# Two-layer cross attention: four context transfers under way instead of eight, one context block in another buffer, a small matrix product placed later

## The chip, the cores and the metric

The kernel runs on one core of one Trainium2 chip, in 32-bit floats. The metric is device time in microseconds (us) of one execution; the median of three executions before the change is 591.29 us (590.97 to 593.39). Engine names are those of the profile: PE multiplies matrices, PEld loads its weights, DVE, ACT and POOL work on vectors, SP issues most of the DMA transfers.

## The reference, cut to what matters

Eight batches (B) of 100 queries (T) with 1024 features (E) attend to a context of 1444 rows (S) with 512 features (L), in two layers one after the other. Layer 0 has an output projection and a softmax over the context; layer 1 has a softmax over the queries, no output projection, and a layer norm.

```python
def _L0_xattn_ref(query, key, Wq, bq, Wk, bk, Wv, bv, Wo, bo):
    Q = jnp.einsum('bqd,dh->bqh', query, Wq) + bq
    K = jnp.einsum('bkd,dh->bkh', key, Wk) + bk
    V = jnp.einsum('bkd,dh->bkh', key, Wv) + bv
    scores = jnp.einsum('bqh,bkh->bqk', Q, K) * scale
    weights = jax.nn.softmax(scores, axis=-1)
    attended = jnp.einsum('bqk,bkh->bqh', weights, V)
    return query + jnp.einsum('bqh,hd->bqd', attended, Wo) + bo

def _L1_xattn_ref(emb, latent, Wq, bq, Wk, bk, Wv, bv, gamma, beta):
    ...
    w = jax.nn.softmax(w, axis=1)
    pred = jnp.einsum('btm,bme->bte', w, v)
    x = pred + emb
    ...
    return (x - mu) * jax.lax.rsqrt(var + EPS) * gamma + beta
```

## The kernel before

**The algebra.** The kernel never forms keys or values. It multiplies Wq by Wk once (qk0 for layer 0, qk1 for layer 1) and Wv by Wo (vo0), with seven half-size products where eight would be plain (`weight_products`, L350). From qk0 and the queries it makes g0T (`queries`, L657), so that the scores of a batch are g0T times the context itself. The weighted context rows A are then projected: `project0` (L1041) after layer 0, `project1` (L1194) and `project_last` in layer 1.

**The context comes twice per batch and layer.** `load_features` (L862) brings it transposed, as four feature blocks cT_b_0 to cT_b_3 of 128 features by 1444 rows, each in two transfers (704 and 740 columns; the page lists them as 352 and 370 KB). `load_rows` (L871) brings it as it lies, as four pieces c_b_0 to c_b_3 of three blocks of 128 rows each: eleven transfers of 256 KB, and for the last 36 rows one of 72 KB and one of 64 KB. So a batch needs 21 transfers. All go through `loaded_in_order` (L859), which issues them on SP's queue in the order of the program. Completion is told by eight semaphores in turn, so each transfer is issued only after the eighth before it has landed: up to eight are under way.

**Buffers.** The pool `stream` (L60) holds ten units; a unit takes one piece c_b_q, or one of the blocks cT_b_0 and cT_b_1. Blocks cT_b_2 and cT_b_3 go to three buffers with the tag prob (`feature_block`, L86). A transfer into a buffer also waits until PE is through with what was in it. Before the context, the units hold the weights for qk1.

**The order on PE** is written out by hand. `scores_by_keys` (L941, matmuls at L957) goes through the four feature blocks of a batch, and in each through the twelve row blocks in the order KEYS (8, 11, 9, 10, 0 to 7), so the second half of a block is wanted first. `weighted_rows` (L902, matmuls at L910) makes A of a batch from the pieces c in order. `alternated` (L1318) runs A of batch b and the scores of batch b+2 step by step in turn; the scores of batches 0 and 1 run ahead of it. The sequence of layer 0 stands at L1330 to L1368: loads for batches 0, 1 and partly 2, the scores of batch 0, further loads, the scores of batch 1, then eight rounds of `alternated`; the first two parts of `project0` run after the seventh round, the rest after the eighth. Layer 1 begins with `queries(1, ...)`, the scores of its batches 0 and 1 (L1394 to L1399), and runs `alternated` in three sets (batches 0 to 3, 4 to 6, and 7) with a projection after each.

**DVE, ACT and POOL** are scheduled by the framework, except where `vector.in_order` or `keep_in_program_order` holds them to the program's order. `softmax0` (L981) and `softmax1` (L1125) work on the scores of one batch while PE is at the next ones.

**The small product.** Layer 1's bias vectors are sums over weights (`block_sums`, L590). `totals("k1", ...)` (L601, matmul at L604) multiplies those partial sums by a matrix of zeros and ones, `same`, to add them over the partitions; DVE then masks and adds (L607, L609). Its results u1 and wqbk1 are used by `queries(1, ...)` (L1355) and `key_bias_sums` (L1373). It stands at L1364, at the end of round b = 1, just ahead of `value_sums` (L1367), which prepares sums of wvo for `project0` on DVE.

Of the kernel before, what the change touches and what calls it, by code (L numbers as in the profile page):

```python
# [34 lines left out]
S, L = 1444, 512  # L35
EC, LC = E // P, L // P
# [13 lines left out]
PAD = S - LAST + QD  # L50
SCALE = 1.0 / math.sqrt(E)
EPS = 1e-6


@with_exitstack
def two_layer_cross_attention(ctx: ExitStack, tc: tile.TileContext, a: dict, out: bass.AP):
    nc = tc.nc
# [10 lines left out]
    def bank(name):  # L68
        return psum.tile([P, 512], F32, tag="ps", name=name)
# [4 lines left out]
    def unit(name):  # L74
        return stream.tile([P, E + L], F32, tag="unit", name=name)

    def wide(name):
        return work.tile([P, LC, GT], F32, tag="AT", name=name, bufs=2)
# [7 lines left out]
    def feature_block(name):  # L86
        return work.tile([P, S], F32, tag="prob", name=name, bufs=3)
# [55 lines left out]
    def run(*parts):  # L143

        parts = list(parts)
        while parts:
            parts = [g for g in parts if next(g, parts) is not parts]
# [442 lines left out]
    def block_sums(name, t, sums, late=False):  # L590

        ins = nc.vector.transpose(t, t)
        if late:
            tc.keep_in_program_order(ins)
        nc.vector.tensor_reduce(sums, t.rearrange("p (c q i) -> p c q i", q=P // QD, i=QD), AX.X, ALU.add)

    def totals(name, sums, n):  # L601

        ps = bank(name)[:, : n * P // QD]
        nc.tensor.matmul(ps, same, sums.rearrange("p c q -> p (c q)"), start=True, stop=True)  # L604
        own = small.tile([P, 2 * EC, P // QD], F32, tag="own", name=f"{name}_own", bufs=1)[:, :n, :]
        mask = quarter.unsqueeze(1).to_broadcast([P, n, P // QD])
        nc.vector.tensor_tensor(own, ps.rearrange("p (c q) -> p c q", q=P // QD), mask, ALU.mult)  # L607
        got = const.tile([P, n], F32, tag=name, name=name)
        nc.vector.tensor_reduce(got, own, AX.X, ALU.add)  # L609
        return got  # L610

    def quarter_sums(name):
        return small.tile([P, 2 * EC, P // QD], F32, tag="sums", name=f"{name}_sums")
# [14 lines left out]
    def key_bias_sums(name, wqbk, tiles=()):  # L628

        acc = to = work.tile([P, B * T], F32, tag="kb", name=name, bufs=1)

        def steps():
            if tiles:
                scaled_sum(tiles, [(xT[:, k, :], wqbk[:, k : k + 1]) for k in range(EC)])
            for k in range(len(tiles), EC):
                if k == len(tiles):
                    vector.tensor_scalar(to, xT[:, k, :], wqbk[:, k : k + 1], None, ALU.mult)  # L640
                else:
                    vector.scalar_tensor_tensor(to, xT[:, k, :], wqbk[:, k : k + 1], to, ALU.mult, ALU.add)
                yield
            if tiles:
                transfer_added(to, tiles[0])

        return acc, steps()
# [178 lines left out]
    for g in range(B // G):  # L826
# [3 lines left out]
                out=xT[:, :, g * GT : (g + 1) * GT],  # L830
                in_=a["xT"].rearrange("(c p) t -> p c t", p=P)[:, :, g * GT : (g + 1) * GT],
# [16 lines left out]
    kb0, more = key_bias_sums("kb0", wqbk0[:, :EC], [t[:, : B * T] for t in prob])  # L848
# [3 lines left out]
    sums = quarter_sums("k1")  # L852
# [3 lines left out]
        tc.keep_in_program_order(nc.scalar.activation(xT[:, e, :], xT[:, e, :], AF.Identity, bias=bias))  # L856


    def loaded_in_order(to, src):  # L859
        tc.keep_in_program_order(nc.sync.dma_start(out=to, in_=src))  # L860

    def load_features(b):  # L862

        for k in range(LC):
            name = f"cT_{b}_{k}"
            t = feature_block(name) if k >= LC // 2 else unit(name)[:, :S]
            for part in (slice(0, LAST // 2), slice(LAST // 2, S)):
                loaded_in_order(t[:, part], a["ctxT"][b][k * P : (k + 1) * P, part])
            yield t

    def load_rows(b):  # L871

        src = a["ctx_512"][b]
        for q in range(NQ):
            t = unit(f"c_{b}_{q}").rearrange("p (c l) -> p c l", c=CQ)
            n = CQ - (q == NQ - 1)
            r0 = q * CQ * P
            for i in range(n):
                loaded_in_order(t[:, i, :], src[r0 + i * P : r0 + (i + 1) * P, :])
            if n < CQ:  # L880
                more = PAD - (S - LAST)
                loaded_in_order(t[: S - LAST, n, :], src[LAST:S, :])
                loaded_in_order(t[S - LAST : PAD, n, :], src[:more, :])
            yield t
# [56 lines left out]
    def scores_by_keys(s, layer, cT, softmax):  # L941

        b = s["b"]
        q = gT[layer][b // G]
        t0 = b % G * T
        banks = [bank(f"s{layer}_{b}_{n}") for n in range(MC // GM)]
        rest = []
        for k in range(LC):
            for m in KEYS:
                whole = keys(m) == P  # L950
                n = HP if whole else keys(m)
                for h in both_sides() if whole else one_side():
                    o = m * P + h * HP if whole else m * P
                    to = banks[m // GM][h * HP : h * HP + n, m % GM * T : (m % GM + 1) * T]
                    if k >= LC - 2 and not whole:
                        rest.append(to)
                    nc.tensor.matmul(  # L957
                        to,
                        cT[k][:, o : o + n],
                        q[:, k, t0 : t0 + T],  # L960
                        start=(k == 0 and m % GM == 0),
                        stop=(k == LC - 1 or (k == LC - 2 and not whole)),
                        skip_group_check=True,
                    )
                if (k, m) != (LC - 1, KEYS[-1]):
                    yield
        w = weight_rows(f"w{layer}_{b}")
        s["w"] = w[:, : MC * T].rearrange("p (c t) -> p c t", t=T)
        nc.gpsimd.memset(s["w"][:PAD, MC - 1, :], 0.0)  # L969
        s["softmax"] = softmax(s, [blocks_of(banks, ms) for ms in ROWS], rest)  # L970
        for _ in islice(s["softmax"], LATER.get((layer, b))):
            pass
        yield
# [257 lines left out]
    def normalise(s):  # L1231
# [6 lines left out]
        rstd = small.tile([T, 1], F32, tag="rstd", name=f"rstd_{b}")  # L1238
        nc.vector.tensor_scalar(rstd, mv[:, 1:2], EPS, None, ALU.add)
        nc.gpsimd.tensor_tensor(rstd, rstd, mhalf[:T], ALU.pow)  # L1240
# [19 lines left out]
    def project_last(s, A, first):  # L1260
# [31 lines left out]
        vector.tensor_tensor(v, sq[:, 0:1], sq[:, 1:2], ALU.add)  # L1292
        vector.tensor_scalar(v, v, 1.0 / E, EPS, ALU.mult, ALU.add)
        for part in parts[1:]:
# [23 lines left out]
    def alternated(b, layer, softmax, dst, first=0, got=None):  # L1318
# [6 lines left out]
        for _ in range(MC * LC):  # L1325
            next(A)
            next(ahead, None)
            yield

    loads = [load_features(b) for b in range(3)]  # L1330
    cT = [list(islice(load, n)) for load, n in zip(loads, (LC, LC - 1, 0))]
    c0 = list(load_rows(0))
    cT[2] += islice(loads[2], LC // 2)
    run(scores_by_keys(batches[0], 0, cT[0], softmax0))
    cT[1] += loads[1]
    cT[2] += islice(loads[2], 1)
    block_sums("u1", acc_u, sums[:, :LC, :], late=True)
    block_sums("wqbk1", acc_c, sums[:, LC : LC + EC, :], late=True)
    run(scores_by_keys(batches[1], 0, cT[1], softmax0))
    cT[2] += loads[2]  # L1340
    for b in range(B):
        dst = A0[b // G][:, :, b % G * T : (b % G + 1) * T]
        steps = alternated(b, 0, softmax0, dst, *((0,) if b else (MC, (c0, cT[2]))))
        if b == B - 2:
            o0 = project0(AS, A0)
            parts = [next(o0), next(o0)]
        if b < B - 1:
            run(steps)
        if b == B - 2:
            vector.in_order = True  # L1350
            for part in parts:
                run(part)
            vector.in_order = False
        if b == B - 1:
            gT[1], queries1 = queries(1, wqk1, u1)  # L1355
            for n, _ in enumerate(steps):
                if n in (7, 11, 15):
                    vector.in_order = True
                    next(queries1)
                    vector.in_order = False  # L1360
        for e in range(2 * b, 2 * b + 2) if 2 * b < EC else ():
            add_out_bias(e)
        if b == 1:
            got = totals("k1", sums[:, : LC + EC, :], LC + EC)  # L1364
            u1, wqbk1 = got[:, :LC], got[:, LC:]
            vector.in_order = True
            AS = value_sums(wvo)  # L1367
            vector.in_order = False  # L1368
# [4 lines left out]
    kb1, more = key_bias_sums("kb1", wqbk1)  # L1373
# [29 lines left out]
    for bs in SETS:  # L1403
        t = wide(f"A1T_{bs[0]}").rearrange("p c t -> p (c t)")[:, : LC * len(bs) * T]
        t = t.rearrange("p (c t) -> p c t", c=LC)
# [42 lines left out]
```

## Time and profile before

| what | value |
|---|---|
| median of three executions | 591.29 us (590.97 to 593.39) |
| profiled execution, its own time | 592.69 us |
| span of its trace, first to last instruction | 590.9 us |
| mean granted TensorE clock | 0.996 |
| PE busy | 575.6 us (97%) |
| DMA, mean over the span | 242 GB/s, 142.95 MB |
| context transfers (c and cT) | 336 of the issues, all on SP's queue |

The profile is of one execution. Busy time is the union of an engine's instructions; matmuls are pipelined, so that their recorded durations overlap. "Idle before" names what ended an engine's idle time: an instruction of another engine, a DMA, or "issue", where the profile shows nothing that it waited for. Queue q1 carries the transfers that SP issues, q0 those of POOL, and q8 and q14 bring instructions to the engines.

### The profile page before, as it was taken

Reading aid. Unit: us, or ns where it says so; the run is one execution under the profiler, and the core shown is the slowest. Engines: PE = TensorE matmul, PEld = TensorE weight load, DVE = VectorE, ACT = ScalarE, POOL = GpSimd, SP = SyncE. Lnnn points to the kernel's source line nnn. Section 1 sums busy time; section 2 is a strip of 40 time slices with the busy share of each in tenths; the row PEclk is TensorE's granted clock in tenths of the full one; section 3 lists DMA queues with packets and bytes.
Section 4 is the critical chain, followed back from the end, with each engine's and each line's share of the span. In section 5 each row is a group of like instructions: output and inputs, shape, how many; then the busy total and the mean of one; then the engine's idle time right before and its main releaser. Section 6 shows DMA issues by size and latency. Waiting matters only on the chain.

```text
span 590.9 us, 17499 instructions
## 1 busy us (share of the span) xinstructions
PE 575.6 (97%) x7470; PEld 497.1 (84%) x7470; DVE 398.9 (68%) x936; ACT 133.1 (23%) x349; POOL 132.2 (22%) x206
## 2 busy tenths in 40 slices
PE   9999999999999899999999999999989999999994
PEld 8887457678899899999997666787989999999992
DVE  1997589879675963966559597867434447654695
ACT  1331421423420112121111000203333302154313
POOL 3110110221211222141223002205722112341052
PEclk9999999999999999999999999999999999999998
DMA  8959989943699999999972607609999992599124
GB/s 271 311 120 328 300 211 295 259 84 84 118 262 355 343 369 359 369 341 378 352 226 58 245 0 269 225 22 381 345 336 347 355 342 72 157 320 308 48 29 84
DMA packets 65097, 142.95 MB, mean 242 GB/s; under 512 B 7549, under 2 KB 12925, under 8 KB 65021
## 3 DMA queue, kind: packets, MB, share of 16 engines
q1 hardware_dynamic: 56574, 117.80, 56.9%
q0 software_dynamic: 8048, 23.57, 19.1%
q8 instruction: 59, 0.97, 0.7%
q10 hardware_dynamic: 398, 0.47, 0.2%
q14 instruction: 18, 0.14, 0.1%
HBM read 121.53 MB, written 6.14 MB: 216 GB/s over the span
## 4 chain that ended last, share of the span: by engine, by line
PE 89%; DMA 6%; issue 2%; POOL 2%; ACT 1%; DVE 0%; POOLq 0%; DVEq 0%
PE A L910 21%; PE s L957 20%; PE qk_x L166 6%; PE g_x L166 5%; PE o_x L166 5%; PE vo_x L166 4%; DMA cT<-in_ctxT 3%; PE o_y L166 3%; DMA c<-in_ctx 3%; PE g_y L166 3%; PE qk_y L166 2%; PE qk_z L166 2%; PE o_w L166 1%; PE o_z L166 1%; PE qk_w L166 1%
## 5 line engine op out<-in xcount | busy, mean ns | idle before, releaser
L910 PE MATMUL A<-w,c 128*64 128x100 f32 (+1 forms) x3072 | 228.4, 249 | 0.9 <-issue 0.9
L910 PEld LDWEIGHTS A<-w,c 128*64 128x64 f32 (+1 forms) x3072 | 198.9, 137 | 4.4 <-issue 4.1
L957 PE MATMUL s<-g1T,cT 128*64 128x100 f32 (+1 forms) x1472 | 114.5, 249 | 2.3 <-issue 2.2
L957 PE MATMUL s<-g0T,cT 128*64 128x100 f32 (+1 forms) x1472 | 112.8, 249 | 3.6 <-DMA cT<-in_ctxT 1.9
L957 PEld LDWEIGHTS s<-g1T,cT 128*64 128x64 f32 (+1 forms) x1472 | 98.5, 136 | 4.7 <-issue 4.0
L957 PEld LDWEIGHTS s<-g0T,cT 128*64 128x64 f32 (+1 forms) x1472 | 96.5, 136 | 4.3 <-DMA cT<-in_ctxT 2.1
L1169 POOL TENSOR_TENSOR part<-w 128x500 f32<-128x500 f32 x16 | 23.8, 1486 | 124.9 <-ACT w L1017 61.9
L1149 ACT ACTIVATE w<-w,negmax 128x100 f32<-128x100 f32 x96 | 35.0, 366 | 71.1 <-DVE negmax L99 71.1
L99 DVE SCALAR_TENSOR_TENSOR w<-s,kb 128x400 f32<-128x400 f32 (+2 forms) x32 | 13.9, 463 | 40.3 <-PE s L957 40.1
L1017 ACT ACTIVATE w<-w 128x400 f32<-128x400 f32 (+2 forms) x32 | 12.0, 442 | 123.0 <-DVE w L99 123.0
L99 DVE TENSOR_REDUCE most<-s 128x100 f32<-128x400 f32 (+1 forms) x24 | 12.5, 522 | 39.7 <-PE s L957 39.6
L166 PE MATMUL qk_x<-qk 128*128 128x256 f32 x128 | 30.2, 384 | 0.0
L166 PEld LDWEIGHTS qk_x<-qk 128*128 128x128 f32 x128 | 23.7, 194 | 3.1 <-ACT qk L440 0.2
L1229 DVE SCALAR_TENSOR_TENSOR z<-vectors,r,z 100x512 f32<-100x512 f32 x16 | 11.4, 743 | 12.5 <-PE z L1227 12.4
L99 DVE TENSOR_TENSOR w<-w,rtotal 128x400 f32<-128x400 f32 (+2 forms) x32 | 18.3, 571 | 1.1
L1242 ACT ACTIVATE z<-z,rstd 100x1024 f32<-100x1024 f32 x7 | 8.1, 1151 | 45.4 <-POOL rstd L1240 45.4
L969 POOL MEMSET w<- 68x100 f32 x16 | 3.8, 238 | 64.1 <-PE A L910 46.2
L1149 ACT ACTIVATION_READ_ACCUMULATOR w<-w,negmax 128x1 f32 x96 | 18.0, 188 | 0.0
L99 DVE TENSOR_TENSOR xT<-xT,o_x 128x400 f32<-128x400 f32 (+1 forms) x32 | 15.9, 538 | 2.7 <-PE o_x L166 2.4
L578 POOL DMA_DIRECT2D qk_L_xattn_bk<-qk_L_xattn_bk x6 | 5.2, 922 | 47.9 <-DMA qk_L_xattn_bk<-qk_L_xattn_bk 19.6
L673 ACT ACTIVATE g1T<-g_x,k 128x400 f32<-128x400 f32 x4 | 2.4, 594 | 59.2 <-PE g_x L166 59.1
L166 PE MATMUL vo_x<-vo 128*128 128x512 f32 x32 | 15.3, 595 | 0.0
(435 smaller groups left out, 1052.3 us busy)
## 6 DMA issues: line engine op xcount, KB each, us to landing
c<-in_ctx SPq DMA_DIRECT2D x176, 256.0 KB, 6.1
cT<-in_ctxT SPq DMA_DIRECT2D x64, 370.0 KB, 6.5
cT<-in_ctxT SPq DMA_DIRECT2D x64, 352.0 KB, 6.1
vo<-in_L_xattn_Wo SPq DMA_DIRECT2D x8, 512.0 KB, 7.6
qk<-in_L_xattn_WqT SPq DMA_DIRECT2D x8, 512.0 KB, 5.9
qk<-in_L_xattn_WqT SPq DMA_DIRECT2D x15, 256.0 KB, 5.0
xT<-in_xT SPq DMA_DIRECT2D x2, 1600.0 KB, 24.3
qk_L_xattn_bk<-qk_L_xattn_bk POOLq DMA_DIRECT2D x6, 512.0 KB, 8.6
```

What stands on the lines that cost most here:

```text
L99: ins = getattr(nc.vector, op)(*args, **kw)
L166: nc.tensor.matmul(banks[n // per][:, n % per * width : (n % per + 1) * width], lhs[i][:, n * P : (n + 1) * P], rhs[i], start=(fresh and i ...
L578: nc.gpsimd.dma_start(out=to, in_=t, accum_op=ALU.add)
L673: nc.scalar.activation(dst[g][:, c, :], banks[j][:, :GT], AF.Identity, bias=u[:, c : c + 1])
L910: nc.tensor.matmul(ps[h * HP : (h + 1) * HP, k * T : (k + 1) * T], c[m // CQ][:r, m % CQ, k * P + h * HP : k * P + (h + 1) * HP], w[:r, m, :],
L957: nc.tensor.matmul(to, cT[k][:, o : o + n], q[:, k, t0 : t0 + T], start=(k == 0 and m % GM == 0), stop=(k == LC - 1 or (k == LC - 2 and no ...
L969: nc.gpsimd.memset(s["w"][:PAD, MC - 1, :], 0.0)
L1017: nc.scalar.activation(rows, rows, AF.Exp)
L1149: nc.scalar.activation(rows[:, i, :], rows[:, i, :], AF.Exp, bias=negmax[:, i : i + 1], accum_out=total[:, i : i + 1])
L1169: add(part, w[:, 0:5, :], w[:, 5:10, :], ALU.add)
L1229: nc.vector.scalar_tensor_tensor(z[:, half], bv1[j][:T], s["r"], ps[:T, :], ALU.mult, ALU.add)
L1242: nc.scalar.activation(z, z, AF.Copy, scale=rstd)
```

## The change

1. `loaded_in_order` keeps a list of the last transfers and makes each wait for the landing of the fourth before it (`UNDER_WAY = 4`). This holds for every context transfer of both layers; other transfers are not limited.
2. `load_features` takes the set of blocks that go to the prob buffers. Batch 1 of layer 0 puts only its block 2 there, and its blocks 0, 1 and 3 into units.
3. The loads at the start of layer 0 change their order. Before: batch 0, blocks 0 to 2 of batch 1, the rows c of batch 0, blocks 0 and 1 of batch 2; after the scores of batch 0 block 3 of batch 1 and block 2 of batch 2; after the scores of batch 1 block 3 of batch 2. Now: batch 0, all of batch 1, the rows of batch 0, block 0 of batch 2; after the scores of batch 0 the blocks 1 to 3 of batch 2. From then on the order of loads is as before.
4. `totals("k1", ...)` moves from round b = 1 to round b = 6, behind the first two parts of `project0`. On PE the one 128x48 matmul moves, on DVE its two operations. The instructions of ACT and POOL keep their order, and all other PE instructions too.

```diff
+UNDER_WAY = 4
...
+    under_way = []
+    landed = mybir.DependencyInfo(mybir.DependencyClass.Sync, mybir.DependencyReason.DATA)
+
     def loaded_in_order(to, src):
-        tc.keep_in_program_order(nc.sync.dma_start(out=to, in_=src))
-
-    def load_features(b):
+
+        load = tc.keep_in_program_order(nc.sync.dma_start(out=to, in_=src)).ins
+        if len(under_way) == UNDER_WAY:
+            tc.add_manual_dep(load, under_way.pop(0).name, landed, reason="few transfers under way")
+        under_way.append(load)
+
+    def load_features(b, blocks=(2, 3)):
 
         for k in range(LC):
             name = f"cT_{b}_{k}"
-            t = feature_block(name) if k >= LC // 2 else unit(name)[:, :S]
+            t = feature_block(name) if k in blocks else unit(name)[:, :S]
...
-    loads = [load_features(b) for b in range(3)]
-    cT = [list(islice(load, n)) for load, n in zip(loads, (LC, LC - 1, 0))]
-    c0 = list(load_rows(0))
-    cT[2] += islice(loads[2], LC // 2)
+    cT = [list(load_features(0)), list(load_features(1, (2,)))]
+    c0, more = list(load_rows(0)), load_features(2)
+    cT.append([next(more)])
     run(scores_by_keys(batches[0], 0, cT[0], softmax0))
-    cT[1] += loads[1]
-    cT[2] += islice(loads[2], 1)
+    cT[2] += more
     block_sums("u1", acc_u, sums[:, :LC, :], late=True)
     block_sums("wqbk1", acc_c, sums[:, LC : LC + EC, :], late=True)
     run(scores_by_keys(batches[1], 0, cT[1], softmax0))
-    cT[2] += loads[2]
...
             for part in parts:
                 run(part)
             vector.in_order = False
+            got = totals("k1", sums[:, : LC + EC, :], LC + EC)
+            u1, wqbk1 = got[:, :LC], got[:, LC:]
...
         if b == 1:
-            got = totals("k1", sums[:, : LC + EC, :], LC + EC)
-            u1, wqbk1 = got[:, :LC], got[:, LC:]
             vector.in_order = True
             AS = value_sums(wvo)
```

## Prediction

> **What bounds the kernel now.** I read the page first, for the shares of the engines and the chain that ended last.
>
> ```profile
> PE 575.6 (97%) x7470; PEld 497.1 (84%) x7470; DVE 398.9 (68%) x936; ACT 133.1 (23%) x349; POOL 132.2 (22%) x206
> q1 hardware_dynamic: 56574, 117.80, 56.9%
> q8 instruction: 59, 0.97, 0.7%
> PE 89%; DMA 6%; issue 2%; POOL 2%; ACT 1%; DVE 0%; POOLq 0%; DVEq 0%
> ```
>
> PE is the bound, so a time can only be gained where PE stands still. The waits of PE, and its timeline at the first scores and in layer 1, say where that is:
>
> ```profile
> PE s L957 <- issue: 3.9, 5, 1.7
> PE s L957 <- DMA cT<-in_ctxT: 1.9, 1, 1.9
> PE A L910 <- issue: 0.9, 3, 0.4
> ```
>
> ```profile
> 184.70 11.59 PE L957 MATMUL s<-g0T,cT 128*64 128x100 f32 x257
> 196.69 3.05 PE L957 MATMUL s<-g0T,cT 128*64 128x100 f32 x65 [0.40 <-issue]
> 201.65 4.17 PE L957 MATMUL s<-g0T,cT 128*64 128x100 f32 x92 [1.91 <-DMA cT<-in_ctxT]
> ...
> 432.12 0.39 PE L957 MATMUL s<-g1T,cT 128*64 128x100 f32 x4 [1.72 <-issue]
> ```
>
> One pause waits for a context transfer (201.65). The others are "issue": the page names nobody. I therefore numbered PE's instructions in the trace (15,179 with weight loads and semaphore waits) and set them beside the 59 packets of queue q8, of 16,384 bytes each. All nine longer "issue" pauses fall on instruction 449 + 256n, where n is the packet that ended last, 1.23 to 1.56 us earlier. So PE has run out of instructions and waits for its next block of 256. Matmul records last 249 ns but follow each other at 43, so a gap hides about 0.2 us of a pause; from start to start I get 6.7 us in the nine pauses and 1.2 in eleven small ones at the same boundaries: 7.9 us, 3.15 of it in layer 0. The cT pause is 2.2 us in the same measure.
>
> Why does a block come late? PE needs 5.42 us for a block (128 matmuls at 42.3 ns). Where no context transfer is under way, the packet of the next block starts at most 0.6 us after PE enters a block (eight cases, some of them ahead of it); I take the entry as the request. With six to eight transfers under way (41 requests) it starts 1.0 to 4.9 us later, 2.6 in the mean; with two to five (five requests) 0.2 to 2.5. It then takes 1.0 us, and 1.4 pass until PE goes on. PE stalls when the start is later than 5.42 - 1.0 - 1.4 = 3.0 us.
>
> The chain of waits before the cT pause, and SP's own waits in layer 0, show the depth of the queue:
>
> ```profile
> 178.38 9.01 DMA c<-in_ctx
> ...
> 187.40 7.40 DMA c<-in_ctx
> ...
> 194.81 6.79 DMA cT<-in_ctxT
> ...
> 201.65 4.17 PE s L957 x92
> ```
>
> ```profile
> SPq L860 <- DMA c<-in_ctx: 26.8, 59, 2.3
> SPq L860 <- DMA cT<-in_ctxT: 11.8, 22, 0.8
> SPq L860 <- PE s L957: 8.0, 8, 2.5
> ```
>
> Each issue waits for the eighth transfer before it, which needs 6 to 9 us to land. Alone, one of 352 KB lands 3.02 us after its issue (133.35 to 136.37), one of 256 KB after 2.80 (507.18 to 509.98); in a row they land 0.92 and 0.66 us apart.
>
> [...]
>
> **The change part by part.**
>
> *Fourth block of batch 1 (cT_1_3) in a stream unit.* Before, it took the prob buffer of cT_0_2 and was issued behind c0, at 192.80 and 194.81; it landed at 201.60, 0.04 us before its use. Now it goes ahead of c0's thirteen transfers and lands in the 180s. Gain 2.2 us. In exchange cT_2_0 has two more transfers ahead of it, 1.84 us. Its second half landed at 198.01 and is needed at 203.67; without the earlier pauses (2.2 + 0.8) need moves to 200.7. It lands at 198.0 + 1.84, plus 1.5 for the window (next part) = 201.35. A new wait of 0.7 us; 0 to 2. The blocks after it follow with 0.3 to 3.6 us to spare. Units of batches 1 to 3 turn by one place and are released long before (waits of 9 to 14 us in the queue).
>
> *Four under way.* Behind each waiting transfer on SP's queue stand only other context transfers. Gain: with at most four issued,[...] one or two lie before the fetch, so it starts 1 to 2 us late: all 7.9 us come back but for 0.5 that I leave for odd cases (0 to 2).
> The price is a bubble in the stream. By hand: a transfer lands at the later of (landing of the fourth before it + its time alone) and (the one before it + its spacing). Runs of c,c,c,cT: 2.90 of spacing against 3.02, so 0.12 lost, three times a batch. Behind c_b's two small transfers (36 and 32 rows, about 0.2 each), the next cT has .66 + .4 + .92 = 1.98 against 3.02: 1.04 lost. That is 1.4 us a batch if nothing fills the bubble; fetches fill part, so 0.4 to 1.4. Does DMA have room? It is busy throughout:
>
> ```profile
> 206.00:312.00 106.00, 104.70 (x2412) 103.97 (x2410) 65.39 (x184) 15.83 (x32) 25.42 (x48) 1.00 0.96 337
> ...
> 397.00:484.00 87.00, 84.31 (x1758) 79.63 (x1755) 38.27 (x98) 23.89 (x124) 30.59 (x47) 1.00 1.01 349
> ```
>
> (last two columns: DMA share, GB/s). A batch lands in 16.7 us in layer 0 (c_1 at 206.31 to c_6 at 289.94, five batches), 17.3 in layer 1 (401.68 to 470.99, four), while PE without pauses needs 376 matmuls, 16.0 us. So the stream already falls behind and lives on its lead. Layer 0: second half of cT_3_0 would land at 210.8 (before 210.16) and is needed at 217.7 (221.30 - 4.3 of pauses + 0.7); 4.75 batches later cT_7_3 lands at 210.8 + 4.75 x (17.1 to 18.1) = 292.0 to 296.8, needed at 300.26 - 5.35 + 0.7 = 295.6: room of 3.6 to -1.2 us. Layer 1: lead 8.7 + 0.6 us at cT_2_0; 3.75 batches later PE's need has moved by 64.3 (413.92 to 478.23) - 3.7 of pauses = 60.6, so the landing may move by 69.9; it moves by 3.75 x (17.7 to 18.7) = 66.4 to 70.1, so 3.5 to -0.2 is left at cT_5_3. The last set starts with loads far ahead (smallest lead 5.98 us, 1.5 batches). I take 0.7 for this, half of the worst; 0 at best.
>
> *0/1 product.* PE's two records (0.29 us each, about 0.3 on its path) stand now beside the first projection: moved, not removed. DVE's two (0.19 each) go to 321, ahead of the layer-1 sums, whose product comes at 359. The value sums (eight of 0.41 us) leave the third batch's softmax, whose weights are wanted some 10 us later. Nothing: covered by those 38 and 10 us; without the cover 0.4 and 3 us.
>
> Sum: -2.2 + 0.7 - 7.9 + 0.5 + 0.7 = -8.2 us. Profiled execution 592.7 (span 590.9): 584.5. Median 591.3: **583.1**. All gain and no price: -10.1, 581.2.
>
> **The rivals.**
> (1) Stream behind: the bubble and the fetches add up, 1.8 to 2.0 us a batch. For it: DMA busy 0.96 to 1.01. Against: fetches fall into bubbles. Layer 0 is late by 4.75 x (16.73 + 1.9) - 84.8 (from 210.8 to 295.6) = 3.7, layer 1 by 3.75 x (17.33 + 1.9) - 69.9 = 2.2; gain 10.1 - 0.7 - 5.9 = 3.5: 587.8.
> (2) The depth of the queue doesn't set the fetch's delay[...]: the 7.9 stay, only cT_1_3 is gained: -2.2 + 0.7, 589.8. Against: the same packets start at once with nothing under way.
> (3) Slower: the window is too narrow. If each transfer must wait for its slowest engine, and each of three fetches a batch (1.0 us) delays one, x = 1.4 + 1.5 = 2.9 us a batch: layer 0 late by 8.5, layer 1 by 6.0, with 0.7 = 15.2 against 10.1: +5.1, 596.4. It decides from x = 2.3. For it: the four in the window are worth 4 x 0.76 = 3.04 us, no more than one's life. Against: the engine that is last still has three queued when the next is issued.
> (4) The window isn't in force: the built order shows it in SP's waits, so under 1 in 100.
>
> **How the numbers follow.** Forecast 0.55, rival 1 0.13, rival 2 0.16, rival 3 0.16. A measurement tells about 0.5% (3 us) from no change: faster is below 588.3. Faster: 0.55 + 0.13 = 0.68; same 0.16; slower 0.16. Own range of the forecast 580.9 to 586. The whole range goes up to rival 2 with its bounds (592) and leaves most of rival 3 out.
>
> **What would show it.** Right: no "issue" pause over 0.3 us on PE, q8's packets within 2 us of their requests, SP's waits on DMA longer while transfers land within 3 to 4 us, no cT wait at the fourth block of batch 1, perhaps one of under 1 us at cT_2_0. Wrong: waits of PE on cT or c near 290 or 465 to 480 (rivals 1, 3), or pauses that stay at the block boundaries (rival 2).

## The result and the profile after

| | before | after |
|---|---|---|
| median of four executions | 591.13 us (590.80 to 593.39) | 627.98 us (625.83 to 634.64) |
| ratio, 95% interval | 1 | 1.0615 (1.0563 to 1.0666) |
| profiled execution, its span | 592.69, 590.9 us | 626.79, 625.0 us |
| mean granted TensorE clock | 0.996 | 0.990 |

The change makes the kernel 6% slower; the forecast was 583.1. Times and ratios, here and below, are of fast runs alone: a few executions come out over 1.5% above the fastest of their kernel and are left out. The page after (busy times, the two DMA queues, the chain that ended last):

```profile
PE 583.8 (93%) x7470; PEld 503.0 (80%) x7470; DVE 400.0 (64%) x936; ACT 133.2 (21%) x349; POOL 134.7 (22%) x206
q1 hardware_dynamic: 56574, 117.80, 56.9%
q8 instruction: 59, 0.97, 0.6%
PE 57%; DMA 36%; DVE 2%; issue 1%; POOL 1%; ACT 1%; SPq 1%; DVEq 0%; POOLq 0%; ACTq 0%
```

The bytes are the same, but DMA has gone from 6% to 36% of the chain. PE's waits after (total us, times, longest):

```profile
PE s L965 <- DMA cT<-in_ctxT: 29.5, 25, 4.1
PE s L965 <- DVE most L100: 1.8, 1, 1.8
PE A L918 <- ACT w L1025: 1.1, 1, 1.1
```

Two things happened at once. The "issue" waits, 4.8 us in five and three pieces before, are gone; in their place stand 25 waits for the transposed context. Lines L965, L918 and L865 are L957, L910 and L860 of before. The queue of SP between 184 and 310 us, the same stretch as in the prediction:

```profile
SPq L865 <- DMA cT<-in_ctxT: 48.3, 45, 2.5
SPq L865 <- DMA c<-in_ctx: 28.1, 60, 2.3
SPq L865 <- PE s L965: 0.8, 1, 0.8
```

SP stands waiting for landings for 76 us instead of 39, and hardly ever for a buffer. What that does to the stream shows in the busy time by stretch (last three columns: granted clock, DMA share, GB/s):

```profile
206.00:312.00 106.00, 91.92 (x1984) 89.65 (x1980) 52.26 (x144) 14.35 (x28) 24.18 (x40) 0.97 0.83 274
...
421.00:510.00 89.00, 78.58 (x1612) 72.90 (x1610) 35.22 (x89) 23.40 (x123) 30.40 (x46) 1.00 0.85 272
```

337 and 349 GB/s have become 274 and 272, so that a batch of context lands in 22.2 us (five batches from 212.48 to 323.42) where it took 16.7. PE needs a batch every 16.0 us. The forecast put this number at 17.1 to 18.7.

Measured from start to start of matmuls as in the prediction (43 ns apart when nothing stops them; pauses over 0.11 us, between 190 and 560 us), pauses at the boundaries of instruction blocks fell from 7.3 to 1.1 us, long waits, nearly all for cT, rose from 2.1 to 37.7, and small pauses rose from 1.6 to 7.5: together +35.3, against +34.1 in the span. The long waits take in two that the profile puts down to another engine: "most" at 261.64, which ended 0.13 us after a block of cT had landed, as the others did, and "w" (1.1 us), which is no wait for cT.

### The profile page after: what moved, and what is told of

The parts are those of the page before. It is cut to its first block, busy times and chain, and to the rows that moved or that the text cites. A ratio compares the mean times of both kernels' runs of the same rounds, so it can differ in the third digit from the quotient of the medians.

```text
span 625.0 us, 17505 instructions
## 1 busy us (share of the span) xinstructions
PE 583.8 (93%) x7470; PEld 503.0 (80%) x7470; DVE 400.0 (64%) x936; ACT 133.2 (21%) x349; POOL 134.7 (22%) x206
## 4 chain that ended last, share of the span: by engine, by line
PE 57%; DMA 36%; DVE 2%; issue 1%; POOL 1%; ACT 1%; SPq 1%; DVEq 0%; POOLq 0%; ACTq 0%
DMA c<-in_ctx 20%; DMA cT<-in_ctxT 16%; PE A L918 6%; PE qk_x L167 6%; PE g_x L167 5%; PE o_x L167 5%; PE s L965 5%; PE vo_x L167 3%; PE o_y L167 3%; PE g_y L167 3%; PE qk_z L167 2%; PE qk_y L167 2%; PE o_w L167 1%; PE o_z L167 1%; PE qk_w L167 1%
## 5 line engine op out<-in xcount | busy, mean ns | idle before, releaser
L918 PE MATMUL A<-w,c 128*64 128x100 f32 (+1 forms) x3072 | 232.2, 251 | 1.3 <-ACT w L1025 1.1
L918 PEld LDWEIGHTS A<-w,c 128*64 128x64 f32 (+1 forms) x3072 | 213.0, 138 | 3.4 <-issue 1.4
L965 PE MATMUL s<-g0T,cT 128*64 128x100 f32 (+1 forms) x1472 | 117.4, 256 | 19.8 <-DMA cT<-in_ctxT 18.0
L965 PE MATMUL s<-g1T,cT 128*64 128x100 f32 (+1 forms) x1472 | 115.0, 250 | 11.4 <-DMA cT<-in_ctxT 11.4
L965 PEld LDWEIGHTS s<-g0T,cT 128*64 128x64 f32 (+1 forms) x1472 | 106.0, 140 | 23.2 <-DMA cT<-in_ctxT 16.0
L965 PEld LDWEIGHTS s<-g1T,cT 128*64 128x64 f32 (+1 forms) x1472 | 102.1, 136 | 15.3 <-DMA cT<-in_ctxT 13.6
L1177 POOL TENSOR_TENSOR part<-w 128x500 f32<-128x500 f32 x16 | 26.4, 1653 | 125.7 <-ACT w L1025 60.5
L579 POOL DMA_DIRECT2D qk_L_xattn_bk<-qk_L_xattn_bk x6 | 5.2, 922 | 47.0 <-DMA qk_L_xattn_bk<-qk_L_xattn_bk 19.3
```

What stands on the lines that cost most here:

```text
L579: nc.gpsimd.dma_start(out=to, in_=t, accum_op=ALU.add)
L918: nc.tensor.matmul(ps[h * HP : (h + 1) * HP, k * T : (k + 1) * T], c[m // CQ][:r, m % CQ, k * P + h * HP : k * P + (h + 1) * HP], w[:r, m, :],
L965: nc.tensor.matmul(to, cT[k][:, o : o + n], q[:, k, t0 : t0 + T], start=(k == 0 and m % GM == 0), stop=(k == LC - 1 or (k == LC - 2 and no ...
L1177: add(part, w[:, 0:5, :], w[:, 5:10, :], ALU.add)
```

## The experiments

The ratio is to the kernel before on the same chip, with its 95% interval. The experiments ran on several chips, on which the kernel before took 592.9 to 593.9 us (591.1 above), so ratios are compared and not times.

**All of the change but the window** (eight under way, as before).

```diff
-UNDER_WAY = 4
+UNDER_WAY = 8
```

> The changed kernel with eight under way instead of four: its other parts alone. Theory (the window of four makes the stream of context too slow, and the rest of the change is small): the 36 us are gone; the pause at the fourth block of batch 1 (2.2 us) is gone too, the pauses at instruction blocks (7.9 us) are back: 588 to 590.5. Rival (the new order of the first loads or the moved product is what costs): above 600.

Measured: 593.30 us, ratio 0.9999 (0.9975 to 1.0022). PE's waits here:

```profile
PE s L965 <- issue: 3.1, 6, 0.9
PE A L918 <- issue: 2.4, 5, 1.0
```

The pause at the fourth block of batch 1 is gone (its last transfer lands 12 us ahead), and still nothing is gained: boundary pauses rose from 7.3 to 8.9 us, as the fetches started 2.8 us after their requests instead of 2.5. In this pair of profiles what the buffer won the fetches took. The time lies above the 588 to 590.5 us that were expected.

**The window alone, in the kernel before.**

```diff
     def loaded_in_order(to, src):
-        tc.keep_in_program_order(nc.sync.dma_start(out=to, in_=src))
+        load = tc.keep_in_program_order(nc.sync.dma_start(out=to, in_=src)).ins
+        if len(under_way) == UNDER_WAY:
+            tc.add_manual_dep(load, under_way.pop(0).name, landed, reason="few transfers under way")
+        under_way.append(load)
```

> The kernel before with the window of four alone. Theory: the window is nearly the whole loss: 624 to 634, with the wait for the fourth block of batch 1 larger than before. Rival (loads in the old order don't suffer): below 600.

Measured: 625.66 us, ratio 1.0520 (1.0469 to 1.0572). Its waits on PE:

```profile
PE s L965 <- DMA cT<-in_ctxT: 32.8, 19, 8.5
```

The window of four makes 5.2 of the 6.2%; whether the rest of the change adds the last per cent cannot be told, as the intervals touch. Its longest wait, 8.5 us, is at the fourth block of batch 1.

**Four under way, but of 722 and 768 KB** (each block of cT in one transfer, each piece of c in one).

```diff
-            for part in (slice(0, LAST // 2), slice(LAST // 2, S)):
-                loaded_in_order(t[:, part], a["ctxT"][b][k * P : (k + 1) * P, part])
+            loaded_in_order(t, a["ctxT"][b][k * P : (k + 1) * P, :])
...
-            for i in range(n):
-                loaded_in_order(t[:, i, :], src[r0 + i * P : r0 + (i + 1) * P, :])
+            loaded_in_order(t[:, :n, :], src[r0 : r0 + n * P, :].rearrange("(i p) l -> p i l", p=P))
```

> The changed kernel, still four under way, but each transfer twice or three times as large: a feature block in one transfer of 722 KB, the three row blocks of a piece in one of 768 KB. Theory: four of these hold as many bytes as eight to twelve of the others, so the queue on each engine stays filled: 584 to 592, and the pauses at instruction blocks are partly back. Rival (it is the number of completions waited for, not the bytes queued): above 600.

Measured: 595.14 us, ratio 1.0019 (0.9995 to 1.0042), a little above the 584 to 592 us expected. PE's waits (L963 and L916 are the lines of the scores and of A here):

```profile
PE s L963 <- issue: 3.5, 6, 0.9
PE A L916 <- issue: 3.3, 4, 1.0
```

Four large transfers behave like eight small ones on PE: no wait for cT, and boundary pauses of 9.7 us, with fetches 2.8 us late in the mean (1.1 behind four small ones). The stream itself is slower than with eight small ones (18.1 us a batch against 16.4), which its lead still covers. So neither the number four nor the wait on SP does the harm, and how long a fetch waits goes with the amount of data under way (bytes or packets: the row packets kept their 2,048 bytes, so the two grow together). The mean DMA share from 206 to 312 us is 0.91 here and 0.83 in the changed kernel; how much each single engine had queued, the traces do not show.

**The stream by itself.** Only the context transfers run, three batches at each window, then four with the two small transfers left out, then four and two large ones. TensorE does next to nothing, and no instruction block is fetched during the stages. Nothing of the reference is computed.

```diff
+STAGES = [(8, '', 1), (8, '', 3), (6, '', 3), (5, '', 3), (4, '', 3), (3, '', 3), (4, 'whole', 3), (4, 'large', 3), (2, 'large', 3)]
+MATMULS = 8
```

> The context transfers alone: nothing is computed, the output is zeros. In stages of three batches, each with its window: 8, 6, 5, 4, 3, then 4 without the two small transfers, then 4 and 2 with large transfers. PE runs 8 matmuls. Theory A (each fetch of PE's instructions delays one DMA engine, and a window of four makes all wait for it): without fetches the window of four streams a batch in 16 to 17.5 us, that of eight in 15. Theory B (four are too few for a transfer's own life, fetches or not): 20 to 22 us for four, 15 for eight.

Measured (mean of the second and third batch of each stage): 16.6 us a batch with eight under way, 17.1 with six, 18.0 with five, 20.4 with four, 23.1 with three; four without the two small transfers 19.3; four large 17.0, two large 24.1. The windows of eight and of four, by stretch:

```profile
54.30:87.40 33.10, 0.00 (x0) 0.00 (x0) 0.00 (x0) 0.00 (x0) 1.00 0.98 347
...
221.10:261.80 40.70, 0.00 (x0) 0.00 (x0) 0.00 (x0) 0.00 (x0) 1.00 0.86 281
```

With nothing else on the core four under way move 281 GB/s and eight 347. Theory B is right about four: the window is too narrow by itself. Eight take 1.6 us more than either theory had.

**The same with TensorE at work.** First with matmuls that all go to the same half of the columns, so that a block of instructions is fetched only every 11 us (12,800 matmuls in a span of 1,102.8 us, where 15,600 on alternating halves, below, took 677.0):

```diff
-MATMULS = 8
+MATMULS = 6400
```

> The same transfers while PE runs matmuls that need none of them (6400, a block of 256 instructions every 5.4 us or so). Theory A: window of four 20 to 22 us a batch, of eight 16.5 to 17.5. Theory B: no more than 1.5 us above the run without PE in each stage.

Measured: 15.9 us a batch with eight, 17.7 with six, 18.9 with five, 21.0 with four, 24.2 with three. Two stretches of a batch or two differ by up to 1 us here, so a cost of 0.6 at four is only a hint, and the run does not decide between the theories. Then with matmuls on alternating halves, a fetch every 5.4 us, and six batches a stage:

```diff
+        h = n % 2 * HP
-        nc.tensor.matmul(ps[:HP, :T], ones[:, :HP], ones[:, :T], start=True, stop=True, skip_group_check=True)
+        nc.tensor.matmul(ps[h : h + HP, :T], ones[:, h : h + HP], ones[:, :T], start=True, stop=True, skip_group_check=True)
```

> The context transfers alone, six batches each with 8, 6, 5, 4 and 3 under way, while TensorE runs matmuls that alternate between the two halves of its columns, so that an instruction block is fetched about every 5.4 us as in the kernel (the load-only kernel had none, the one with slower matmuls one in 11 us). It computes nothing of the reference. Slowest-engine theory (rival 3 of the prediction): each fetch costs a narrow window about 1 us and a wide one little, so four needs 20.4 + 3.9 x (0.5 to 1) = 22.4 to 24.3 us a batch and eight 16 to 17. Life theory: four needs 20.4 to 21.6 whether or not there are fetches, and five 18 to 19.3.

Measured: 16.5 us a batch with eight, 18.5 with six, 20.1 with five, 22.35 with four, 26.0 with three. The stretches of eight and of four:

```profile
56.20:138.40 82.20, 80.97 (x1877) 80.46 (x1874) 0.00 (x0) 0.00 (x0) 1.00 1.01 360
...
397.30:509.00 111.70, 111.70 (x2609) 111.70 (x2606) 0.00 (x0) 0.00 (x0) 1.00 0.83 269
```

Against the stream with TensorE idle, eight under way lose nothing and four 1.9 us a batch, 0.47 us for each of 4.1 fetches. These are single runs on two chips, and TensorE's work comes together with its fetches, so this comparison alone does not prove the fetches guilty. The run with a fetch every 11 us helps, as it was made on the chip of the idle one: with four under way, the 28 transfers during whose life a block was fetched had 1.44 us between the first and the last of their 16 landing updates, the 32 others 0.91 (1.11 with TensorE idle). In the changed kernel it is 1.60 for 54 such transfers and 0.92 for 26 others. A longer life also meets a fetch more often, so part of this is selection; but TensorE's work without a fetch adds nothing here (0.91 against 1.11). Four and five come out above what the life theory expected, and four just at the lower edge of the slowest-engine one. In time, both hold a part: of the 5.9 us between four and eight, 3.8 are there without any fetch (20.4 against 16.6), and the rest comes with the run that has them.

**Other widths.** The changed kernel with six, seven and five.

```diff
-UNDER_WAY = 4
+UNDER_WAY = 7
```

> Six under way. Theory: what counts is how much is queued on the slowest of the DMA engines when a transfer is issued; with five ahead the stream needs about 17 us a batch again, while an instruction block waits for fewer transfers: 583 to 589. Rival (a transfer's life grows with the number under way, and each step from eight costs in proportion): between the two ends, 600 to 612.

> The changed kernel with seven transfers under way. If the window trades fetch pauses against the speed of the stream, this lies between eight (pauses at the block boundaries 8.2 us, no wait for cT) and six (3.5 us of pauses, 7.0 us of waits for cT, ratio 0.988): boundary pauses 5 to 6.5 us, waits for cT 0 to 2, ratio 0.988 to 0.995. If only the transfers' count mattered for fetches (a step between six and eight), it equals one of the two.

> The changed kernel with five under way. Theory (life of a transfer sets the stream): in the load-only kernel five need 18.0 to 19.0 us a batch against 20.4 to 21.3 for four; with what the kernel adds (22.3 against 20.8) 19.5 to 20. The 5.6 us a batch that four lose over 8.5 batches are 48 us, of which 33 became waits, so a lead of 15; five lose 3 x 8.5 = 25 - 15 = 10 us, less 7 of fetch pauses: 592 to 598 us, ratio 1.00 to 1.01. Rival (each fetch delays the whole window, whatever its width): close to four, above 610.

Measured: six 586.66 us, ratio 0.9877 (0.9834 to 0.9920); seven 585.34 us, 0.9858 (0.9817 to 0.9900); five 601.44 us, 1.0127 (1.0087 to 1.0167). Seven beats both kernels by 1.4%, with an interval clear of 1; six and seven cannot be told apart. The boundary pauses of seven, 2.8 us, are fewer than the 5 to 6.5 expected, so it isn't a step half-way between eight and six. The waits on PE with seven, besides the first weights:

```profile
PE s L965 <- issue: 1.4, 3, 0.6
PE A L918 <- issue: 0.3, 1, 0.3
```

Neither kind of wait is left in size. Five was expected at 592 to 598 and came out later still: a batch lands every 19.5 us, and the waits for cT come to 16.2 us rather than 10.

**Is the rest of the change worth anything at these widths?** The kernel before with a window of six and of seven, and the changed kernel with seven but the 0/1 product back in round b = 1.

```diff
         if b == 1:
+            got = totals("k1", sums[:, : LC + EC, :], LC + EC)
+            u1, wqbk1 = got[:, :LC], got[:, LC:]
             vector.in_order = True
```

> The kernel before with a window of six and nothing else of the change. If the fourth block of batch 1 in a stream unit is worth anything once fetches come early, this is slower than six in the changed kernel (ratio 0.988) by its pause at the fourth block of batch 1, 2 to 4 us: 0.991 to 0.996. If the buffer and the moves are worth nothing, 0.986 to 0.990.

> The kernel before with a window of seven alone. If the fourth block of batch 1 in a stream unit is worth what the prediction gave it (2.2 us) once fetches no longer absorb it, this is slower than seven in the changed kernel (ratio 0.986) by about 2 us: 0.988 to 0.991, with one wait of 1.9 to 3 us at 202 us. If the rest of the change is worth nothing, 0.984 to 0.988 and no such wait.

> The changed kernel with seven under way and the 0/1 product back in round b = 1. The prediction gave its move nothing: ratio 0.984 to 0.988, as with the move (0.986). If the two vector operations or the product on the path of PE counted, 0.990 or more.

Measured: before with six 588.78 us, ratio 0.9911 (0.9876 to 0.9945); before with seven 588.38 us, 0.9923 (0.9895 to 0.9951); the changed kernel with the product back 586.06 us, 0.9896 (0.9849 to 0.9942). The last two ran side by side and differ by 2.3 us, which fits the buffer of the fourth block (and the order of the first loads, which goes with it): before with seven has one long wait for cT, 2.4 us at 200.6, and the other has none. The intervals overlap, so the trace carries this more than the times do. The product's move cannot be told from nothing: 0.9858 with it and 0.9896 without, with intervals that overlap, though the second lies between the two expectations.

All widths together (pauses by the measure above; "late" is the start of a fetch after its request while context transfers are under way, mean and longest; a dash stands where no number was taken):

| under way | rest of the change | ratio | us a batch, layer 0 | fetch late, us | pauses at boundaries, us | other waits over 0.15, nearly all for cT, us |
|---|---|---|---|---|---|---|
| 8 | no (before) | 1 | 16.7 | 2.5, 4.9 | 7.3 | 2.1 |
| 8 | yes | 0.9999 | 16.4 | 2.8, 4.3 | 8.9 | 0 |
| 7 | no | 0.9923 | 16.9 | 2.3, 3.7 | 2.7 | 2.4 |
| 7 | yes | 0.9858 | 17.0 | 2.3, 3.8 | 2.8 | 0 |
| 6 | no | 0.9911 | 18.2 | 1.9, 3.7 | 1.3 | 3.9 |
| 6 | yes | 0.9877 | 18.5 | - | - | - |
| 5 | yes | 1.0127 | 19.5 | 1.5, 3.5 | 0.3 | 16.2 |
| 4 | yes (after) | 1.0615 | 22.2 | 1.1, 3.0 | 1.1 | 37.7 |
| 4 | no | 1.0520 | 22.0 | 1.1, 2.8 | 0.9 | 37.1 |
| 4 large | yes | 1.0019 | 18.1 | 2.8, 4.6 | 9.7 | 0 |

Fetches come earlier with every transfer taken from the window, and the stream slows with it. Down to seven the first matters: PE has 3.0 us of patience (the prediction's 5.42 - 1.0 - 1.4, an estimate from the trace of the kernel before), and a mean of 2.3 leaves few fetches beyond it. At six the second barely shows (all but 0.5 of the 3.9 us stand at the fourth block of batch 1), and from five on it outweighs the first.

## Why the prediction was wrong

**Fetches: right.** The forecast was that all but 0.5 of 7.9 us come back; 1.1 of 7.3 stayed (the second measure counts pauses over 0.11 us alone), and no fetch started more than 3.0 us late while the context streamed (1.1 in the mean). That one or two of four transfers lie before a fetch was the author's estimate; no trace shows it. Rival 2 (the depth does not set the delay) falls by the table: the delay follows the amount under way, 2.8 us behind four transfers of about 750 KB and 1.1 behind four of half that size or less.

**The fourth block of batch 1: right in size.** 2.2 us were forecast and the pause at 201.65 is gone. In the time it shows, if at all, where fetches do not eat it: 2.3 us with seven under way, within the noise, and nothing with eight.

**The new wait at cT_2_0: the place right, the size wrong.** 0.7 us (0 to 2) was forecast, from a landing at 201.35; it landed at 204.31 and PE waited 4.1 us. The 1.5 us granted "for the window" were too few, by the same error as the next step: with eight under way and all else as changed the block landed at 201.24, so the window cost it some 3.1 us.

```profile
184.31 16.04 PE L965 MATMUL s<-g0T,cT 128*64 128x100 f32 x368
204.44 1.90 PE L965 MATMUL s<-g0T,cT 128*64 128x100 f32 x19 [4.09 <-DMA cT<-in_ctxT]
```

**The price of the window: this step failed.** The prediction let a transfer land at "the later of (landing of the fourth before it + its time alone) and (the one before it + its spacing)", and got "0.12 lost, three times a batch" in the runs of c,c,c,cT, and 1.04 behind the small ones. The wrong term is the time alone. With n transfers under way in the mean, a batch of 21 takes 21/n of a mean life, issue to landing. Alone a life was 2.80 to 3.02 us; in the changed kernel it was 4.15 (the 84 transfers of batches 3 to 6 of layer 0) with 3.93 under way, and 21/3.93 x 4.15 = 22.2 us, the measured interval. In the stream without fetches it was 3.85 with 3.97 under way, and 20.4 results. This is bookkeeping; that the longer life is due to the company is what the two stream kernels show.

Where the extra life comes from: the trace shows 16 landing updates for each transfer (13 for the one of 36 rows, which is left out here). The first 256 KB transfer of a stage of the stream kernel, with nothing ahead of it, had its first update 2.2 to 2.5 us after the start of its issue, and its sixteenth 0.2 to 0.5 after the first (seven stages). With four under way and no fetch these are 2.80 and 1.11 us, in the changed kernel 2.80 and 1.38. The updates come separately, and the next issue goes out 0.02 us after the last of them (median of the context issues in the changed kernel). The last two are much of the matter: in the changed kernel the fourteenth comes 0.71 us after the first and the sixteenth at 1.38 (mean of 80 transfers); in the stream without fetches 0.75 and 1.11, with them 0.79 and 1.42. So in the runs with fetches the fourteenth update is about as early as in the one without (0.71 and 0.79 against 0.75), and the sixteenth 0.3 us later. Which DMA engine an update belongs to, and why the updates lie 1.11 us apart without fetches, the traces do not tell; that part stays open.

In numbers, a batch: 15.0 us is the sum of the spacings (11 x 0.66 + 8 x 0.92 + 0.4, the last the prediction's estimate for the two small ones; in the kernel before they land 0.40 and 0.21 us after the transfer ahead, medians); a window of four makes it 20.4; with fetches it is 22.35 in the stream kernel, and the changed kernel has 22.2. Of the 5.4 us between 15.0 and 20.4 the two small transfers explain 0.7 (leaving them out saves 1.1, of which 0.4 are their own spacing), less than the 1.04 forecast; the runs between them, priced at 0.36 a batch, cost 4.7 (19.3 measured without the small ones, against 14.6 for the spacings of the other 19). Even eight under way lose 1.6 against the spacings.

**The stream late: the method right, the input wrong.** With 22.2 us a batch the prediction's own sum would have had cT_7_3 land 4.75 x 22.2 = 105 us after cT_3_0 (second halves); it was 104.5 (217.79 to 322.27), with cT_3_0 itself 7 us late against the 210.8 forecast. PE needed it at 295.6 by the forecast's count. Layer 1 forecast that the landing may move by 69.9 us from cT_2_0 to cT_5_3; it moved by 81.5 (431.67 to 513.14), 11.6 too many.

**The rivals.** Rival 3 was what happened, in place and sign, and in mechanism as far as the traces go (the next issue follows the last of 16 updates; that this is the slowest engine's is not shown), at nearly twice its price: x was 5.5 us a batch and not 2.9, past its deciding point of 2.3; its 596.4 us still fall 31.6 short. The waits named as its sign are there, at 289.71 and from 464.29 to 480.66. Its fetch part was near (1.5 forecast for three fetches a batch; 0.47 each makes 1.4), its part without fetches was not (1.4 against 3.8). What stood against it was one sentence, that "the engine that is last still has three queued when the next is issued", which no trace had shown. The stream kernel speaks against that: the DMA engines are busy 0.86 of the time in the mean with four under way and 0.98 with eight, so some stand idle for a part of it, though the trace does not name them. Rival 1, the same addition at 1.8 to 2.0 us a batch, was too small in the same way. The prediction had the warning on its page: it found the stream's room gone at 18 us a batch, and four transfers worth 3.04 us against a life of 3.02, no reserve for any spread at all.

**The 0/1 product: right**, worth nothing that shows.

## What to carry to other kernels

Here a window on transfers had to hold more than the life of one transfer in company, which is read from a run with the window in force and not from a transfer alone: the spacing was 0.7 to 0.9 us, a life of 2.8 to 3.0 alone became one of 3.9 to 4.2 with four under way, and going from six to five cost 2.5%, from five to four 4.9%. A queue that was too deep cost as well, on a path where one does not look for it (instruction fetches 2.5 to 2.8 us late behind 2.3 to 3 MB of data), so its depth is a size to be swept: eight to seven gained 0.8% in the kernel before and 1.4% with the rest of the change, eight to four lost 5 to 6%. When a wait is removed and the time stays, compare the other waits before calling the removal worthless.

## What was not expected of the hardware

Two of PE's long waits cost twice. After the waits that ended at 204.44 and 301.84 (PE idle for 4.09 and 3.26 us) the granted clock, the third number from the end, was about half for some 5.3 and 3.4 us of work, but not after one of 3.24 us that ended at 279.59:

```profile
204.40:210.40 6.00, 5.96 (x80) 5.99 (x82) 5.58 (x17) 0.00 (x0) 0.66 (x3) 0.56 0.92 301
279.60:285.60 6.00, 5.70 (x126) 5.53 (x128) 2.37 (x5) 0.00 (x0) 0.18 (x1) 1.00 0.87 280
301.80:305.40 3.60, 3.56 (x44) 3.56 (x46) 0.00 (x0) 0.00 (x0) 0.00 (x0) 0.53 0.78 239
```

In the two slow stretches 105 matmuls took 8.7 us, where 43 ns each would make 4.5: 4.2 us lost, most of the growth in small pauses. These three waits show no one length of idleness that brings it: the half clock began at 202.88, inside the first wait and 2.5 us after PE's last matmul, and at 301.87, 3.3 us after it, in the second, while 3.24 us brought none. The two low stretches of the clock lasted 6.8 and 3.4 us, waiting included. The prediction had no term for this.
